# A selective scan on one core: two alternating sum banks, a delta preparation that borrows the idle one, and column sums with a standing vector of ones

## The chip, the core and the metric

The kernel runs on one core of one Trainium2 chip. The metric is the device time of one execution in microseconds, as the median of several runs. All float work is fp32 unless said otherwise; a few operands are fp8 or bf16. The engines are named as the profile names them: PE (matrix multiply) and PEld (its weight loads), DVE (vector), ACT (scalar), POOL (gpsimd) and SP (which issues nearly all DMAs). Each engine works through its own queue in the order of the program; semaphores order the engines against each other.

## The reference, cut to what matters

The input is an image batch of 4 x 64 x 64 x 96. Layer 0 normalizes it by groups, projects it to 192 channels with binarized weights, convolves, and then runs a selective scan over 4 directions for each image; layer 1 is a linear attention and a quantized feed-forward. Two parts are touched here. The first is the group mean, which needs the sum over all 4096 positions of each of 96 channels:

```python
m = jnp.mean(g, axis=(1, 2, 4), keepdims=True)      # inside _gn
return ((g - m) / jnp.sqrt(s + eps)).reshape(v.shape)
```

The second is the scan, for each image `b`, direction `k`, channel `d` (192) and state `n` (16), along 4096 positions:

```python
delta = jax.nn.softplus(delta + delta_bias[None, :, :, None])
dA = jnp.exp(dt[..., None] * A[None])
h = dA * h + (dt * ut)[..., None] * Bt[:, :, None, :]
y = jnp.einsum('bkdn,bkn->bkd', h, Ct)               # the sum over the 16 states
```

## The kernel before, in words

**Pieces.** The scan is cut into 1,536 pieces: 4 images x 4 directions x 4 chunks of 1024 positions x 6 groups of 32 channels x 4 quarters of 4 states. A piece is a tile of 128 rows (32 channels x 4 states) by 1024 positions. `Scans.run` (from line 1323) goes through the pieces with one loop; iteration `i` writes out, in this order, the instructions below, and each engine keeps its share of them in that order.

- `loads(i)`: SP issues broadcast loads of delta and delta times u (`dl`), and of the rows of B and C (`bc`), for later pieces.
- `carry(i-1)` (line 1271, ACT): the last column of piece i-1 is kept for the next chunk.
- `evacuate(i-4)` (line 1316, ACT, only when `i % 8 == 3`): the sums of the eight pieces 8m to 8m+7 are copied out of the bank `y` to `ys`, and four stores follow later.
- `decay(i+1)` (line 1231, ACT): exp(delta A) of the next piece, into `dA`, a pool of two buffers in the accumulator memory. Each buffer is free again when the piece two places back has been read.
- `reduce(i-3)` (lines 1302 and 1307, PE): eight recorded matmuls with `sum4` add the states of piece i-3 into the bank `y`; at the last quarter of a group up to two other directions are added too. A tile `y` collects eight pieces. The next tile takes the same bank, so `reduce(8m+8)` needs `evacuate` of the tile before.
- `inject(i+4)` (POOL): w = (delta u) B for the piece four places on, into one of nine buffers.
- `late_product()` and `scan(i)`: the recurrence is one DVE instruction, either in place in `dA` or, when the product with C is to be POOL's, into a buffer `h`. The product with C is DVE's or POOL's; a running tally of both engines' estimated work (`Tally`, line 389 on) decides which when the program is written. Both go through the helper line 401, so the profile tells them apart by tile names.
- One step of each open generator in `lanes`, then one step of `back`.

**Preparing delta.** Every eighth iteration (`i % 8 == 0`) opens one `prepare()` (from line 1149): delta and delta times u for a third of a chunk. Its steps, one in each iteration, are: eight matmuls into the bank `dps` (line 1167); Abs and Relu on ACT (1172, 1173); Exp and Ln on ACT (1175, 1176), Ln writing back into `dps`; the matmul that adds the Relu part (1179); the product with u on DVE; a copy on ACT (1185) and the stores. It also issues the load of u into `pu` (line 1157). Three preparations run ahead of the loop in borrowed tiles (`w_s`, `dA_s`).

**Banks.** The pool `ps` has four one-bank tiles: `y`, `dps`, and `b0`, `b1`, which `back` uses. The pool `dA` has the other half of the accumulator memory.

**What stands around the loop.** The weights are made (`weights`) in turns with the first image's `prologue` before the loop. `back` yields the rest of that prologue, then the prologues of the other images, the transposes of one direction (`turn`) and the attention and feed-forward of each finished image (`Epilogue`), one step in each iteration. The last image's epilogue runs after the loop.

**Column sums.** At the start of `prologue` 32 matmuls (line 510, two records each) take a block of x, 128 positions by 96 channels, as standing weights and a single column of ones as moving data; they add up in one column `csum`. Four steps hold eight matmuls each. Then ACT copies the column (514), a matmul adds the three channels of a group (`gsum`, 516), and ACT makes the negative mean (519).

Of the kernel before, what the change touches and what calls it, by code (L numbers as in the profile page):

```python
# [53 lines left out]
def hybrid_kernel(ctx: ExitStack, tc: tile.TileContext, a: dict, out: bass.AP):  # L54
# [102 lines left out]
    def weights():  # L157
# [28 lines left out]
        def transposed(dst, srcs):  # L186

            count[0] += 1
            ps = p.ps.tile([128, 1024], BF16, name=f"tps{count[0]}", tag=("y", "dps")[count[0] % 2])
            at = 0  # L190
            for src in srcs:
                n, f = src.shape
                nc.tensor.transpose(ps[:f, at : at + n], src, identb[:n, :n])
                at += n
            nc.vector.tensor_copy(dst, ps[:f, 0:at], saturate=False if dst.dtype == F8 else None)
# [152 lines left out]
        nc.vector.tensor_copy(  # L348
            back4.rearrange("p (x d) -> p x d", x=4), ident.rearrange("p (x d) -> p x d", x=4)[:, ::-1, :]
        )  # L350
        ps = p.ps.tile([128, 512], F32, name="tpd", tag="dps")
        for g in range(3):
            for x in range(4):
                nc.tensor.matmul(
# [122 lines left out]
def prologue(c, b, xts=None):  # L477
# [5 lines left out]
    def f32(nm):  # L483
        return p.f.tile([128, 512], F32, name=f"{nm}_{b}", tag="f")
# [4 lines left out]
    with tc.tile_pool(name=f"xg_{b}", bufs=1) as xgp:  # L489
# [3 lines left out]
        with tc.tile_pool(name=f"cv_{b}", bufs=1) as cvp:  # L493
# [6 lines left out]
            if xts is None:  # L500
# [4 lines left out]
                load_x(c, b, xts)  # L505
                yield
                yield
            csum = bank("csum", 0)[0:96, 0:1]
            for i in range(NT):
                nc.tensor.matmul(csum, xts[i // 8][:, i % 8, :], c.ones1, start=(i == 0), stop=(i == NT - 1))  # L510
                if i % 8 == 7:
                    yield
            cs = f32("cs")[0:96, 0:1]
            nc.scalar.copy(cs, csum)
            gsum = bank("gsum", 1)[0:96, 0:1]
            nc.tensor.matmul(gsum, c.grp, cs, start=True, stop=True)
            yield
            negm = f32("negm")[0:96, 0:1]
# [578 lines left out]
class Scans:  # L1097
# [19 lines left out]
    def done(self, b, n):  # L1117

        return self.at > (b * NK + n) * NPC + SETTLE


    def load_signs(self, b, k):

# [6 lines left out]
    def prepare(self, spare=None):  # L1130

        nc, c, p = self.c.nc, self.c, self.c.p
        b, k, ci, part = self.todo.pop(0)
        nm = f"{b}_{k}_{ci}_{part}"

        at = 16 * (NCH - 1 - ci if k >= 2 else ci)
        if (b, k) not in self.gs:  # L1140
            self.load_signs(b, k)
        if (ci, part) == (NCH - 1, 0) and k != KORD[-1]:
            self.load_signs(b, KORD[KORD.index(k) + 1])
        ud = (c.utd if k % 2 else c.ud)[b].rearrange("h p (n l) -> (h p) n l", l=IW)
        if part != 1:
            u = spare[2] if spare else p.pu.tile([128, CH], F32, name=f"pu_{nm}", tag="pu")
            if part == 0:
                cuts = ((slice(0, 128), slice(0, 128), slice(at, at + 16)),)
            else:
                lines = [slice(at + 8 * x, at + 8 * x + 8) for x in range(2)]  # L1150
                cuts = [
                    (slice(64 * x, 64 * x + 64), slice(128, DN), lines[1 - x if k >= 2 else x]) for x in range(2)
                ]
            n = 16 if part == 0 else 8
            v = u[:, 0 : 64 * n].rearrange("p (n l) -> p n l", l=IW)
            for rows, chans, lines in cuts:
                nc.sync.dma_start(v[rows], ud[chans, lines])
            self.us = v[:, ::-1, ::-1] if k >= 2 else v
        gT = self.gs[b, k]
        uv = self.us[:, 8 * part : 8 * part + 8] if part < 2 else self.us  # L1160
        d = spare[0] if spare else p.pd.tile([128, 2, 512], F32, name=f"pd_{nm}", tag="pd")
        ps = spare[3] if spare else p.ps.tile([128, 512], F32, name=f"dps_{nm}", tag="dps")
        pv = ps.rearrange("p (c q s) -> p s q c", q=4, s=8)
        groups = ((0, 128, 0, part),) if part < 2 else ((0, 64, 128, 0), (64, 64, 128, 1))
        wd, c0 = (c.wdz, 32 * ci + 16 * part) if part < 2 else (c.wdy, 32 * ci)
        for s in range(8):
            nc.tensor.matmul(pv[:, s], wd[:, k, s], gT[:, :, c0 : c0 + 16], start=(s == 0), stop=(s == 7))  # L1167
        yield
        kind = part // 2
        sc, bi = c.pvd[:, kind, k : k + 1], c.dbias[:, kind, k : k + 1]  # L1170
        t = spare[1] if spare else p.pd.tile([128, 512], F32, name=f"sp_{nm}", tag="sp", bufs=1)
        nc.scalar.activation(d[:, 0], ps, AF.Abs, scale=sc, bias=bi)  # L1172
        nc.scalar.activation(t, ps, AF.Relu, scale=sc, bias=bi)  # L1173
        yield
        nc.scalar.activation(d[:, 0], d[:, 0], AF.Exp, scale=-1.0)
        nc.scalar.activation(ps, d[:, 0], AF.Ln, bias=1.0)
        yield

        nc.tensor.matmul(ps, c.ident, t, start=False, stop=True, skip_group_check=True)  # L1179
        yield  # L1180
        c.vec.tensor_tensor(
            d[:, 1].rearrange("p (i j) -> p i j", j=64), ps.rearrange("p (i j) -> p i j", j=64), uv, ALU.mult
        )
        yield
        nc.scalar.copy(d[:, 0], ps)
        for x, (r0, n, d0, hf) in enumerate(groups):
            at = CH * ci + 512 * hf
            dst = c.dld[k][b][:, d0 : d0 + n, at : at + 512].rearrange("t d l -> d t l")
            then = (lambda: self.loaded.add((b, k, ci, part))) if x == len(groups) - 1 else None
            c.later.store(dst, d[r0 : r0 + n], after=1, then=then)  # L1190
# [102 lines left out]
    def reduce(self, i):  # L1293

        c = self.c
        b, e, ci, g, q = self.pieces[i]
        if i % 8 == 0:
            self.ydone[i // 8] = c.p.ps.tile([128, 2, 256], F32, name=f"yp_{i}", tag="y")
        y, prod = self.ydone[i // 8], self.ins.pop(i)
        more = self.sums.pop(i // NQ, []) if q == NQ - 1 else []  # L1300
        for x in range(4):
            c.nc.tensor.matmul(  # L1302
                y[32 * x : 32 * x + 32, g % 2, :], c.sum4, prod[:, 256 * x : 256 * x + 256],
                start=(q == 0), stop=(q == NQ - 1 and not more), tile_position=(0, 32 * x),
            )
        for n, (src, w) in enumerate(more):
            c.nc.tensor.matmul(y[:, g % 2, :], w, src, start=False, stop=(n == len(more) - 1))  # L1307
# [15 lines left out]
    def run(self, back):  # L1323
        c, lanes, n = self.c, [], len(self.pieces)

        w = [c.p.w.tile([128, CH], F32, name=f"w_s{x}", tag="w") for x in range(7)]
        ps = [c.p.dA.tile([128, CH], F32, name=f"dA_s{x}", tag="dA") for x in range(2)]
        for x in range(3):
            half = slice(512 * (x % 2), 512 * (x % 2) + 512)
            lanes.append(  # L1330
                self.prepare((
                    w[x].rearrange("p (t l) -> p t l", t=2), w[3 + x // 2][:, half], w[5 + x // 2], ps[x // 2][:, half],
                ))
            )
        interleave(lanes)
        for q in range(NQ):
            self.load_bc(0, self.bt, 0, 0, 0, q)
            self.load_bc(1, self.ct, 0, 0, 0, q)
        while lanes:
            interleave(lanes)  # L1340
            c.later.tick()
        c.later.flush()
        self.load_dl(0)
        for m in (1, 2):
            self.load_dl(m)
        self.decay(0)
        for i in range(AHEAD):
            self.inject(i)
        for i in range(n):
            self.at = i  # L1350
            self.loads(i)
            if i % NQ == 1:
                while KORD[self.pieces[i][1]] == 2 and self.pieces[i][0] not in c.turned:
                    next(back)
                self.load_sums(i)
            if i >= 1:
                self.carry(i - 1)
            if i % 8 == 3 and i > 8:
                self.evacuate(i - 4)
            if i + 1 < n:  # L1360
                self.decay(i + 1)
            if i >= 3:
                self.reduce(i - 3)
            if i + AHEAD < n:
                self.inject(i + AHEAD)
            self.late_product()
            self.scan(i)
            c.later.tick()
            if i % 8 == 0 and self.todo:
                while (self.todo[0][0], self.todo[0][1] % 2) not in c.ready:  # L1370
                    next(back)
                lanes.append(self.prepare())
            interleave(lanes)
            next(back, None)
            if i > n - 64:
                next(back, None)
        self.late_product()
        for i in range(n - 3, n):
            self.reduce(i)
        self.evacuate(n - 1)  # L1380
        c.later.flush()
        self.at = 2 * n
# [76 lines left out]
```

## Time and profile before

| | us |
|---|---|
| median of 6 runs | 5537.71 |
| lowest and highest of them | 5531.88 and 5540.85 |
| the profiled execution, its own time | 5541.11 |
| its span in the profile | 5539.3 |
| first scan starts, last scan starts (in the span) | 262.8 and 5414.9 |
| mean granted PE clock, share of full speed | 0.713 |

The profile is one execution. A group of the profile is a line, an engine, an operation and its tiles; it gives the busy time, the mean duration of one, and the idle time of that engine just before, with the event that ended it. The view of waits adds that idle time up by who waited for whom. The timeline gives single instructions with their start and duration in us. The table of windows gives the busy time of each engine in a stretch of the span.

### The profile page before, as it was taken

The page shows a single profiled execution, that of the slowest core. Times are in us where ns is not written, and L with a number is a line of the kernel's source. Part 1 is how long each engine was busy: PE and PEld are TensorE (multiplying, and loading weights), DVE is VectorE, ACT ScalarE, POOL GpSimd, SP SyncE. Part 2 cuts the span into 40 slices and gives each one's busy share as a digit, 9 for nine tenths or more (in the row PEclk, how much of TensorE's full clock was granted, in tenths as well). Part 3 has the DMA queues.
Part 4 walks back from the last instruction along what each step waited for, and adds up shares of the span by engine and source line. Part 5 has one row for each costly group of instructions (what it writes and reads, how often), then busy time and mean ns, then how long its engine had stood idle before and what let it go on. Part 6 is the DMA issues. An engine that isn't in the chain of part 4 may idle for free. (4 is left out here: it accounts for less than half of the span.)

```text
span 5539.3 us, 62371 instructions
## 1 busy us (share of the span) xinstructions
PE 3435.8 (62%) x20197; PEld 1357.9 (25%) x20197; DVE 5051.7 (91%) x3237; ACT 3556.4 (64%) x5564; POOL 4994.1 (90%) x2262
## 2 busy tenths in 40 slices
PE   6456655576557766568656775544676564444677
PEld 3222222222223222223222222111232121111223
DVE  3299999999999999899999999999999999999984
ACT  4467776777666667677766667755566775555554
POOL 2199999899999999899999999999999999999981
PEclk8667776678668876667777777656787776556777
DMA  4455666766666566767656556665665566665642
GB/s 80 124 184 191 206 198 194 250 200 200 210 211 196 192 203 206 222 207 219 205 191 205 189 194 207 218 204 192 216 215 187 187 200 201 212 208 189 206 151 60
DMA packets 613245, 1069.94 MB, mean 193 GB/s; under 512 B 225084, under 2 KB 343925, under 8 KB 611125
## 3 DMA queue, kind: packets, MB, share of 16 engines
q1 hardware_dynamic: 599428, 1065.88, 61.6%
q8 instruction: 159, 2.61, 0.2%
q10 hardware_dynamic: 13488, 0.07, 0.1%
q14 instruction: 170, 1.38, 0.1%
HBM read 833.20 MB, written 229.38 MB: 192 GB/s over the span
## 5 line engine op out<-in xcount | busy, mean ns | idle before, releaser
L401 POOL TENSOR_TENSOR w<-dl,bc 128x1024 f32<-128x1024 f32 x1536 | 3578.8, 2354 | 166.5 <-PE yp L1302 90.5
L1231 ACT ACTIVATE dA<-dl,anm 128x1024 f32<-128x1024 f32 x1536 | 1715.7, 1117 | 472.0 <-DVE w L401 289.5
L1302 PE MATMUL yp<-w,sum 128*32 128x256 f32 x12288 | 1260.2, 507 | 1083.8 <-ACT ys L1316 609.7
L401 DVE TENSOR_TENSOR_SCAN dA<-dA,cy,w 128x1024 f32<-128x1024 f32 x706 | 1654.4, 2343 | 95.0 <-ACT dA L1231 83.9
L401 POOL TENSOR_TENSOR w<-h,bc 128x1024 f32<-128x1024 f32 x596 | 1401.6, 2352 | 96.1 <-DVE h L401 88.4
L401 DVE TENSOR_TENSOR w<-dA,bc 128x1024 f32<-128x1024 f32 x940 | 1151.3, 1225 | 48.4 <-DMA bc<-bcd 0.8
L401 DVE TENSOR_TENSOR_SCAN h<-dA,cy,w 128x1024 f32<-128x1024 f32 x446 | 1043.3, 2340 | 9.7 <-ACT dA L1231 9.0
L1302 PEld LDWEIGHTS yp<-w,sum 128*32 128x32 f32 x12288 | 307.9, 127 | 2132.8 <-issue 688.4
L1271 ACT COPY cy<-dA 128x1 f32<-128x1 f32 x707 | 110.8, 157 | 691.6 <-DVE w L401 690.2
L401 DVE TENSOR_TENSOR_SCAN dA<-dA,w 128x1024 f32<-128x1024 f32 x234 | 534.2, 2283 | 21.9 <-ACT dA L1231 18.1
L577 PE MATMUL cv<-tp,cw 96*96 96x512 fp8e5 x1152 | 362.1, 458 | 80.3 <-ACT r L627 68.0
L401 DVE TENSOR_TENSOR_SCAN h<-dA,w 128x1024 f32<-128x1024 f32 x150 | 341.7, 2279 | 24.0 <-POOL w L401 23.5
L1179 PE MATMUL dps<-sp,ident 128*128 128x512 f32 x378 | 356.1, 1041 | 0.0
L1307 PE MATMUL yp<-ya,back 128*128 128x256 f32 x576 | 234.2, 527 | 0.0
L577 PEld LDWEIGHTS <-cw 96*96 96x96 fp8e5 x1152 | 158.8, 146 | 272.8 <-issue 218.8
L1271 ACT COPY cy<-h 128x1 f32<-128x1 f32 x445 | 82.7, 186 | 147.0 <-DVE h L401 146.0
L847 PE MATMUL yc<-eys,mean 96*96 96x512 f32 x240 | 135.7, 718 | 36.2 <-DVE vks L401 16.0
L1172 ACT ACTIVATE pd<-dps,dbias,pvd 128x512 f32<-128x512 f32 x189 | 143.8, 761 | 15.8 <-PE dps L1167 15.7
L1307 PEld LDWEIGHTS yp<-ya,back 128*128 128x128 f32 x576 | 121.9, 244 | 126.4 <-issue 96.2
L1173 ACT ACTIVATE sp<-dps,dbias,pvd 128x512 f32<-128x512 f32 x189 | 144.7, 766 | 0.0
L401 DVE TENSOR_TENSOR pd<-dps,pu 128x512 f32<-128x512 f32 x189 | 127.5, 675 | 5.1 <-PE dps L1179 4.8
L1316 ACT COPY ys<-yp 128x512 f32<-128x512 f32 x192 | 111.7, 582 | 29.3 <-PE yp L1307 18.7
(282 smaller groups left out, 4028.9 us busy)
## 6 DMA issues: line engine op xcount, KB each, us to landing
dl<-dld SPq DMA_DIRECT2D x768, 512.0 KB
bc<-bcd SPq DMA_DIRECT2D x512, 512.0 KB
dld<-pd SPq DMA_DIRECT2D x126, 512.0 KB
yd<-ys SPq DMA_DIRECT2D x768, 64.0 KB
dld<-pd SPq DMA_DIRECT2D x126, 256.0 KB
ya<-yd SPq DMA_DIRECT2D x192, 128.0 KB
pu<-ud SPq DMA_DIRECT2D x32, 512.0 KB
pu<-utd SPq DMA_DIRECT2D x31, 512.0 KB
```

The lines of the kernel that those rows point to most:

```text
L401: return getattr(self.eng, name)(out, *args, **kw)
L577: nc.tensor.matmul(ps, c.cw[:, j, t, 96 * h : 96 * h + 96], tpad[j][:, 8 * q + dy : 8 * q + dy + 8, dx : dx + IW], start=(j == 0 and t == ...
L847: self.c.nc.tensor.matmul(ps, w, x, start=(i == 0), stop=(i == len(pairs) - 1))
L1172: nc.scalar.activation(d[:, 0], ps, AF.Abs, scale=sc, bias=bi)
L1173: nc.scalar.activation(t, ps, AF.Relu, scale=sc, bias=bi)
L1179: nc.tensor.matmul(ps, c.ident, t, start=False, stop=True, skip_group_check=True)
L1231: c.nc.scalar.activation(t, self.dlt[i // NQ][0], AF.Exp, scale=c.anm[:, g, NQ * KORD[e] + q : NQ * KORD[e] + q + 1])
L1271: self.c.nc.scalar.copy(self.carries[g, q], h[:, CH - 1 : CH])
L1302: c.nc.tensor.matmul(y[32 * x : 32 * x + 32, g % 2, :], c.sum4, prod[:, 256 * x : 256 * x + 256], start=(q == 0), stop=(q == NQ - 1 and no ...
L1307: c.nc.tensor.matmul(y[:, g % 2, :], w, src, start=False, stop=(n == len(more) - 1))
L1316: c.nc.scalar.copy(t, y[:, :, ::-1] if k >= 2 else y)
```

## The change

- The tags `y` and `dps` become `y0` and `y1`. The sums of eight pieces go to `y0` and `y1` in turns (`i // 8 % 2`). `prepare` puts its `dps` tile into the bank that the sums do not use at that time (`bank()`).
- A preparation opens at `i % 8 == 3` and not at 0. It has one empty step more, after Exp and Ln, so that its last step (copy and stores) falls six iterations after its first.
- `evacuate(i-4)` is written after `decay(i+1)`; before, it was written ahead of it.
- A fourth preparation runs ahead of the loop, after the three first `dl` loads are issued and before `decay(0)`, in the tiles `w[7]`, half of `w[4]`, a `pu` tile and half of `ps[1]`.
- The column sums take the ones as standing weights (128 x 1) and 384 columns of x as moving data: eight matmuls in place of 32, two in each of four steps, into a row of 384. ACT copies the row, four small matmuls turn and add its four quarters into one column (`cst`), and a further step follows before `cs` is copied.
- In `weights`, the transposes and the `tpd` tile take `y0` and `y1` in turns.

```diff
-            ps = p.ps.tile([128, 1024], BF16, name=f"tps{count[0]}", tag=("y", "dps")[count[0] % 2])
+            ps = p.ps.tile([128, 1024], BF16, name=f"tps{count[0]}", tag=f"y{count[0] % 2}")
...
-            csum = bank("csum", 0)[0:96, 0:1]
-            for i in range(NT):
-                nc.tensor.matmul(csum, xts[i // 8][:, i % 8, :], c.ones1, start=(i == 0), stop=(i == NT - 1))
-                if i % 8 == 7:
+            csum = bank("csum", 0)[0:1, 0 : 4 * DM]
+            for i in range(0, NT, 4):
+                nc.tensor.matmul(
+                    csum, c.ones1, xts[i // 8][:, i % 8 : i % 8 + 4, :].rearrange("p i e -> p (i e)"),
+                    start=(i == 0), stop=(i == NT - 4),
+                )
+                if i % 8 == 4:
                     yield
+            row = f32("csr")[0:1, 0 : 4 * DM]
+            nc.scalar.copy(row, csum)
+            ps = bank("cst", 1)[0:96, 0:1]
+            for i in range(4):
+                nc.tensor.matmul(
+                    ps, row[:, DM * i : DM * i + DM], c.ones1[0:1, :], start=(i == 0), stop=(i == 3)
+                )
+            yield
             cs = f32("cs")[0:96, 0:1]
-            nc.scalar.copy(cs, csum)
-            gsum = bank("gsum", 1)[0:96, 0:1]
+            nc.scalar.copy(cs, ps)
+            gsum = bank("gsum", 0)[0:96, 0:1]
...
+    def bank(self):
+
+        return max(0, self.at - 3) // 8 % 2
...
-        ps = spare[3] if spare else p.ps.tile([128, 512], F32, name=f"dps_{nm}", tag="dps")
+        ps = spare[3] if spare else p.ps.tile([128, 512], F32, name=f"dps_{nm}", tag=f"y{1 - self.bank()}")
...
         nc.scalar.activation(ps, d[:, 0], AF.Ln, bias=1.0)
+        yield
         yield
...
-            self.ydone[i // 8] = c.p.ps.tile([128, 2, 256], F32, name=f"yp_{i}", tag="y")
+            self.ydone[i // 8] = c.p.ps.tile([128, 2, 256], F32, name=f"yp_{i}", tag=f"y{i // 8 % 2}")
...
-        w = [c.p.w.tile([128, CH], F32, name=f"w_s{x}", tag="w") for x in range(7)]
+        w = [c.p.w.tile([128, CH], F32, name=f"w_s{x}", tag="w") for x in range(8)]
...
+        u = c.p.pu.tile([128, CH], F32, name="pu_s", tag="pu")
+        for _ in self.prepare((w[7].rearrange("p (t l) -> p t l", t=2), w[4][:, 512:CH], u, ps[1][:, 512:CH])):
+            pass
         self.decay(0)
...
+            if i + 1 < n:
+                self.decay(i + 1)
             if i % 8 == 3 and i > 8:
                 self.evacuate(i - 4)
-            if i + 1 < n:
-                self.decay(i + 1)
...
-            if i % 8 == 0 and self.todo:
+            if i % 8 == 3 and self.todo:
```

More of the change, by code (lines that the diff above doesn't have):

```diff
@@ L350, in weights @@
         )
-        ps = p.ps.tile([128, 512], F32, name="tpd", tag="dps")
+        ps = p.ps.tile([128, 512], F32, name="tpd", tag="y0")
         for g in range(3):
```

## The prediction

> **What bounds the kernel now.** I read the page's busy times first, then the windows, the waits of DVE and of POOL inside the loop, and last the timeline. The first two fences are the page's first part and two rows of the table of windows (start and end, length, busy us of PE, PEld, DVE, ACT, POOL, PE clock, DMA share, GB/s).
>
> ```profile
> PE 3435.8 (62%) x20197; PEld 1357.9 (25%) x20197; DVE 5051.7 (91%) x3237; ACT 3556.4 (64%) x5564; POOL 4994.1 (90%) x2262
> ```
>
> ```profile
> 600.00:1600.00 1000.00, 624.61 (x4146) 258.14 (x4144) 957.57 (x588) 708.39 (x1098) 960.81 (x420) 0.70 0.67 206
> 1600.00:2600.00 1000.00, 679.05 (x3718) 257.89 (x3718) 954.94 (x596) 691.81 (x1089) 956.85 (x418) 0.73 0.65 205
> ```
>
> In the loop DVE and POOL are both busy 96% of the time; PE and ACT are not full. So the change, which removes no DVE or POOL work from the loop, can only win idle time of these two. The next two fences are the view of waits of DVE and of POOL between 400 and 5300 us (total us, times, longest).
>
> ```profile
> DVE dA L401 <- ACT dA L1231: 97.8, 84, 5.3
> ...
> DVE dA L401 <- ACT cy L1271: 9.8, 12, 1.3
> DVE h L401 <- ACT dA L1231: 8.2, 6, 3.2
> ...
> DVE dA L401 <- POOL w L401: 2.3, 5, 1.3
> ```
>
> ```profile
> POOL w L401 <- PE yp L1302: 77.2, 50, 6.9
> POOL w L401 <- DVE h L401: 76.0, 100, 2.0
> ```
>
> DVE waits for POOL 2.3 us in 4900, but for a late decay on ACT 97.8 + 8.2 = 106 us. POOL waits for PE 77.2 us and for DVE 76.0 us: it catches up, then waits for DVE again. So DVE sets the loop's time, and a stall of POOL costs nothing while DVE has injected pieces in stock. The price list of the change is what it does to those 106 us.
>
> The groups' view names a larger number, which is not on that path:
>
> ```profile
> L1302 PE MATMUL yp<-w,sum 128*32 128x256 f32 x12288 | 1260.2, 507 | 1083.8 <-ACT ys L1316 609.7
> ```
>
> PE stands 609.7 us before `reduce`, waiting for `evacuate`. What that does to DVE shows in the timeline (start, duration):
>
> ```profile
> 1001.40 1.08 ACT L756 COPY yh<-yt 96x512 f32<-96x512 f32 x1 [2.88 <-DMA yt<-yd]
> 1002.38 0.15 ACT L1271 COPY cy<-dA 128x1 f32<-128x1 f32 x1
> 1002.43 0.58 ACT L1316 COPY ys<-yp 128x512 f32<-128x512 f32 x1
> 1002.91 1.12 ACT L1231 ACTIVATE dA<-dl,anm 128x1024 f32<-128x1024 f32 x1
> ...
> 1003.07 1.08 PE L1302 MATMUL yp<-w,sum 128*32 128x256 f32 x8 [10.88 <-ACT ys L1316]
> ...
> 1004.14 2.35 DVE L401 TENSOR_TENSOR_SCAN h<-dA,cy,w 128x1024 f32<-128x1024 f32 x1 [2.17 <-ACT dA L1231]
> ```
>
> ACT is late, evacuates, and only then makes the decay that DVE waits for: 0.58 of DVE's 2.17 us is the evacuation. PE's 10.88 us delay nobody here.
>
> **Evacuation behind the decay.** I numbered the scans of the timeline and sorted DVE's waits for a decay by piece number modulo 8. Piece 4, whose decay stands behind the evacuation, has 27 of them and 26.2 us, the most of all. Eleven show the pattern above without a wait of ACT's own; each can win at most the copy's 0.58 us or its whole stall, together 6.0 us. In four more the evacuation itself waited (for PE or a load), and the whole stall goes: 0.66 + 0.79 + 0.82 + 0.99 = 3.3 us. In seven, 8.1 us together, the decay began only at the very end of the scan ahead of it (ACT's idle there ends with "DVE h"); an earlier decay may or may not escape that. I take half, 4.0 us. Sum: 6.0 + 3.3 + 4.0 = -13.3 us; bounds 0 (something else on ACT is late next) and -26.2.
>
> **Preparation moved by three iterations, with one step more.** It issues the same instructions: eight matmuls (0.29 us each), Abs and Relu 0.76 + 0.77, Exp and Ln 0.62 + 0.60, two matmul records of 1.04, a DVE product of 0.68, a copy of 0.58. Before, Abs to Ln stand in iterations 1 and 2, just before the evacuation in 3; afterwards the evacuation comes first and Abs to Ln stand in 4 and 5. Piece 3's stalls were 17.9 us, pieces 5, 6, 7 and 0 average 9.7 us; the excess of some 8 us should move to pieces 6 and 7. I take 0, bounds -8 and +8. The `pu` load, one of 512 KB or two of 128, now queues on SP behind two `dl` loads of 512 KB in the same iteration (those come at every `i % 4 == 3`). Its reader is the product five iterations later, 5 x 3.37 = 17 us, before four; DVE waited for `pu` 0.2 us in all. Cost 0.
>
> **Banks.** `reduce(8m+8)` no longer waits for the evacuation. But the preparation's first matmuls, in the same iteration, do: their bank is the one being emptied. PE's queue stops one instruction later, and the evacuation ends later by the decay's 1.12 us. Behind the stop were one reduce (1.08) and the 2.08 us of the Relu matmul; now eight matmuls of 1.03. So `reduce(8m+9)` comes some 1.08 + 2.08 - 1.12 - 1.03 = 1.0 us earlier, and POOL's 77.2 us should shrink, perhaps by half. DVE does not wait for POOL: 0, bounds 0 and -77.2. The new wait's queue: behind it on PE stand the step of `back` and later reduces; ACT's Abs, one iteration on, waits for these matmuls. Between evacuation and Abs ACT has at least a carry and a decay, 0.16 + 1.12 = 1.28 us, against 1.03 on PE. Taken as 0, bounds 0 and +30 (third rival).
>
> The Trainium skill ("Perfetto Trace Analysis", section Matmuls) says that independent groups of matmuls should rotate through banks so that an evacuation overlaps the next group. By that rule the 609.7 us were the prize, and the time 4931 us; by the waits of DVE above it is worth almost nothing, and I go by the waits.
>
> **Start of the loop.** The fourth preparation stands ahead of `decay(0)`. Its chain on its own is 1.0 + 1.5 + 1.2 + 1.8 + 0.7 + 0.6 = 6.8 us, but its product waits for a `pu` load behind six `dl` loads: 7 x 0.524 MB at 247 GB/s (window 253 to 262) from 254 us, so about 269. `decay(0)` comes at about 270 instead of 258.5, and the first scan at 271 instead of 262.8. The cover is POOL: its six injects run from 260.4 to 274.2, and only then does it take the first product. Cost 0; +4 if the load lands that much later.
>
> **Column sums.** Before, 64 records took 10.35 us at the start (31.87 to 42.22) and 4 x 2.7 in the loop. A 384-column fp32 record is not in the trace; a 512-column one is 0.445 us near the end and 1.04 in L1179's mean, so 0.33 to 0.78 for 384, and 5.3 to 12.5 us for 16 of them. At the start the gain is hidden: ACT's `negm` came at 44.26 us, 2 us after the sums, behind a weight step that waits for DMA and POOL. The longer chain (row copy about 0.5, eight short records, one step) puts the prologue one turn behind the weights; turns follow each other by some 1.3 us there (two copies of 0.67). I take +1.3 us, bounds -3 and +4. In the loop one late `csum` held ACT 8.4 us and DVE 5.3 us, once; that stays or goes: 0, bounds -5 and +3.
>
> **The sum.** -13.3 + 1.3 = -12.0 us on the profiled execution's 5541.1: 5529.1. That execution was 3.4 us above the median of 5537.7, so I predict 5526.
>
> **Rivals.**
> 1. *Nothing that can be measured (5538).* PE's wait moves from `reduce` to the preparation, and the decays are late for other causes: half of piece 4's stalls are not behind an idle-free evacuation. For it: the 8.1 us above. Against it: the order on ACT certainly changes. Gain 3 to 5, cost 1.3 to 4.
> 2. *More (5505).* Half of POOL's 77.2 us and the 12 us above come through, 5538 - 39 - 12 = 5487 at most; two thirds of it give 5505. For it: POOL is busy 96% as well and may bind in some stretches. Against it: DVE's 2.3 us.
> 3. *Slower: the stop of PE reaches ACT (5569).* Where ACT is late (27 of 192 blocks), PE starts the preparation 1.12 us later, Abs waits for it in the middle of ACT's queue, and the next decays wait behind Abs: 27 x 1.12 = 30 us, and no gain, +1.3. It decides once PE needs more than 1.28 us from evacuation to Abs; eight matmuls take 1.03 at the slow clock, so 0.25 us are left. Today Abs waits 15.8 us in all.
>
> **Numbers.** Forecast 0.45 (its own range 5512 to 5538), nothing 0.23, more 0.12, slower 0.20. What a measurement of this kernel can tell from no change is about 0.2%, 11 us. Faster by more than that (below 5526.6): 0.28 of the forecast and all of "more", 0.40; within it: 0.17 and 0.23, 0.40; slower 0.20. The range 5503 to 5566 leaves out half of "more" and some 0.12 of "slower".
>
> **What would show it.** Right: PE's wait for `ys` before L1302 falls from 609.7 us to under 60 and returns before L1167; DVE's waits at piece 4 fall from 26 us to 10 to 15; L1172's idle time stays under 40 us; POOL's wait for `yp` falls below 60; the first scan starts at about 271 us, the first product of POOL still near 274. Wrong: waits of DVE for decays at pieces 5 to 7 grow by as much as piece 4 loses (rival 1); L1172 waits 100 us or more for L1167 (rival 3); the loop starts later than 266 us on POOL.

## The result, and the profile after

The changed kernel takes 5553.99 us (median of 16 runs, 5547.84 to 5563.64), the kernel before 5538.58 us beside it (34 runs): ratio 1.0029, 95% interval [1.0022, 1.0035]. It is slower, by 15.4 us. The prediction said 5526 us, 12 us less than before. Its range, 5503 to 5566, holds the time, but only because the third rival had stretched it upwards, and that rival's mechanism did not occur (below). Its sign is wrong.

The profiled execution took 5548.84 us, with a span of 5547.1 us, 5 us below its kernel's median; that of before was 2.5 us above its own. So the profiles show only 7.7 of the 15.4 us (5547.1 - 5539.3). Line numbers after the change: decay 1248, carry 1288, evacuation 1333, `reduce` 1319, the preparation's matmuls 1183, Abs 1188, Relu 1189, Exp 1191, Ln 1192.

The page's first part, and the two windows (start and end, length, busy us of PE, PEld, DVE, ACT, POOL, PE clock, DMA share, GB/s):

```profile
PE 3463.0 (62%) x20037; PEld 1363.5 (25%) x20037; DVE 5053.1 (91%) x3237; ACT 3567.2 (64%) x5568; POOL 4996.1 (90%) x2262
```

```profile
600.00:1600.00 1000.00, 627.83 (x4091) 259.78 (x4089) 957.60 (x590) 709.86 (x1098) 960.41 (x419) 0.71 0.67 207
1600.00:2600.00 1000.00, 669.97 (x3680) 249.21 (x3679) 952.40 (x592) 691.88 (x1086) 955.70 (x418) 0.72 0.65 204
```

DVE, ACT and POOL are busy as before, to 0.3 points. The work did not change; only waits did. The mean granted PE clock was 0.707, against 0.713 before; DVE's waits that PE ended came to 16.6 us between 400 and 5300 us, against 18.9 before, so the clock did not carry the loss there. DVE's and POOL's waits between 400 and 5300 us:

```profile
DVE dA L401 <- ACT dA L1248: 99.4, 87, 3.7
DVE h L401 <- ACT dA L1248: 17.6, 9, 5.3
DVE dA L401 <- ACT cy L1288: 7.0, 8, 1.3
DVE dA L401 <- POOL w L401: 7.0, 7, 1.9
```

```profile
POOL w L401 <- DVE h L401: 106.1, 125, 2.9
POOL w L401 <- PE yp L1319: 46.9, 35, 4.4
```

DVE's wait for decays has grown, from 106.0 to 117.0 us (first two lines). POOL's wait for PE fell from 77.2 to 46.9 us, and its wait for DVE rose by as much, from 76.0 to 106.1. The groups of PE and of Abs (busy us, mean ns of one | idle us before them, and what ended it); the last line is Abs in the kernel before:

```profile
L1319 PE MATMUL yp<-w,sum 128*32 128x256 f32 x12288 | 1299.5, 518 | 448.9 <-POOL w L401 289.2
L1183 PE MATMUL dps<-gT,wdz 128*128 128x64 fp8e5 x1000 | 119.0, 323 | 444.1 <-ACT ys L1333 412.4
L1183 PE MATMUL dps<-gT,wdy 128*128 128x64 fp8e5 x504 | 56.7, 311 | 186.5 <-ACT ys L1333 186.5
L1188 ACT ACTIVATE pd<-dps,dbias,pvd 128x512 f32<-128x512 f32 x188 | 143.2, 762 | 18.1 <-PE dps L1183 17.9
...
L1172 ACT ACTIVATE pd<-dps,dbias,pvd 128x512 f32<-128x512 f32 x189 | 143.8, 761 | 15.8 <-PE dps L1167 15.7
```

`reduce` no longer stands for the evacuation (`ys`); the preparation's matmuls do, for 412.4 + 186.5 = 598.9 us. Abs waits 17.9 us for them, 15.7 before: PE's stop does not reach ACT.

**Where the time came from.** I summed DVE's idle time between scan 64 and the last scan from the timeline: 160.8 us before, 168.5 after, with DVE busy 4776.5 and 4777.7 us (idle time of less than 0.15 us at a stretch is counted as busy). The difference, 7.7 us, is as much as the span grew. The row that grew on ACT's side is its wait, ahead of a decay, for a scan into `h`; here before and after:

```profile
ACT dA L1231 <- DVE w L401: 272.1, 159, 2.8
ACT dA L1231 <- DVE h L401: 144.4, 118, 2.7
```

```profile
ACT dA L1248 <- DVE w L401: 279.6, 167, 2.9
ACT dA L1248 <- DVE h L401: 190.3, 150, 2.7
```

The second row rose from 144.4 us in 118 waits to 190.3 in 150. A timeline of after shows such a wait (start, duration; scan 637 is the one at 2416.59, into `h`):

```profile
2414.87 0.76 ACT L1188 ACTIVATE pd<-dps,dbias,pvd 128x512 f32<-128x512 f32 x1
2415.45 1.23 DVE L401 TENSOR_TENSOR w<-dA,bc 128x1024 f32<-128x1024 f32 x1
...
2416.59 2.34 DVE L401 TENSOR_TENSOR_SCAN h<-dA,cy,w 128x1024 f32<-128x1024 f32 x1
...
2417.52 0.15 ACT L1288 COPY cy<-dA 128x1 f32<-128x1 f32 x1
...
2418.96 1.12 ACT L1248 ACTIVATE dA<-dl,anm 128x1024 f32<-128x1024 f32 x1 [1.29 <-DVE h L401]
...
2420.18 2.36 DVE L401 TENSOR_TENSOR_SCAN dA<-dA,cy,w 128x1024 f32<-128x1024 f32 x1 [1.25 <-ACT dA L1248]
```

ACT is not late: after the carry at 2417.52 it has nothing ahead of decay 638, and stands 1.29 us until scan 637 has ended, at 2418.93. Then the decay takes 1.12 us, and DVE stands 1.25 us. Piece 636 was scanned in place and its product (2415.45) was done at 2416.68, so 636's `dA` buffer was free. But the program gave decay 638 the buffer of 637, the piece *just ahead*, which is read until 2418.93. The semaphore value that this decay waits for in the built program is the one that scan 637 raises.

I call these decays **tied**: the decay of piece k has the buffer of piece k-1 where k-2 is in place and k-1 goes into `h`. Then k-2's buffer always comes free first, since its product stands ahead of scan k-1 on DVE. The built program of before has 73 tied decays, that of after 93; only 22 pieces are tied in both. In the traces 63 and 88 of them begin within 0.08 us of the end of scan k-1, and DVE stands 54.4 and 79.6 us behind them. DVE's other waits for decays fell from 56.8 to 39.6 us. So -17.2 + 25.2 = +8.0 us: the other waits shrank by more than the forecast gain, and the tied decays grew by more than that. (A wait has one last cause, so part of the first is only the second in its place.)

### The profile page after: what moved, and what is told of

Its sections match the earlier page's. It is cut to its first block, busy times and chain, and to the rows that moved or that the text cites. A ratio compares the mean times of both kernels' runs of the same rounds, so it can differ in the third digit from the quotient of the medians.

```text
span 5547.1 us, 62051 instructions
## 1 busy us (share of the span) xinstructions
PE 3463.0 (62%) x20037; PEld 1363.5 (25%) x20037; DVE 5053.1 (91%) x3237; ACT 3567.2 (64%) x5568; POOL 4996.1 (90%) x2262
## 5 line engine op out<-in xcount | busy, mean ns | idle before, releaser
L1319 PE MATMUL yp<-w,sum 128*32 128x256 f32 x12288 | 1299.5, 518 | 448.9 <-POOL w L401 289.2
L401 DVE TENSOR_TENSOR_SCAN h<-dA,cy,w 128x1024 f32<-128x1024 f32 x447 | 1045.8, 2340 | 18.5 <-ACT dA L1248 17.9
L401 DVE TENSOR_TENSOR_SCAN dA<-dA,w 128x1024 f32<-128x1024 f32 x235 | 536.6, 2283 | 34.1 <-ACT dA L1248 28.1
L1183 PE MATMUL dps<-gT,wdz 128*128 128x64 fp8e5 x1000 | 119.0, 323 | 444.1 <-ACT ys L1333 412.4
L1196 PE MATMUL dps<-sp,ident 128*128 128x512 f32 x376 | 273.5, 817 | 60.2 <-ACT dps L1192 60.2
L1183 PEld LDWEIGHTS <-wdz 128*128 128x128 fp8e5 x1024 | 99.4, 156 | 526.8 <-issue 491.7
L1183 PE MATMUL dps<-gT,wdy 128*128 128x64 fp8e5 x504 | 56.7, 311 | 186.5 <-ACT ys L1333 186.5
L1188 ACT ACTIVATE pd<-dps,dbias,pvd 128x512 f32<-128x512 f32 x188 | 143.2, 762 | 18.1 <-PE dps L1183 17.9
```

What stands on the lines that cost most here:

```text
L401: return getattr(self.eng, name)(out, *args, **kw)
L1319: c.nc.tensor.matmul(y[32 * x : 32 * x + 32, g % 2, :], c.sum4, prod[:, 256 * x : 256 * x + 256], start=(q == 0), stop=(q == NQ - 1 and no ...
```

## The experiments

The first theory is that: the buffers that the pool `dA` hands out set the time; the change moves instructions on ACT, and with them the choice made when the program is written. The rivals: one part of the change costs by itself, through ACT's queue (the swap, the later preparation, the banks), or through the start (the column sums, the fourth preparation). Each expectation names its theories anew. The table behind the experiments gathers their numbers.

**1 and 2. Fixed buffers, in the kernel before and in the kernel after.** Each piece has the buffer of its parity, so no decay can be tied. (The other users of the pool get one of the two tags as well.)

```diff
-        t = c.p.dA.tile([128, CH], F32, name=f"dA_{i}", tag="dA")
+        t = c.p.dA.tile([128, CH], F32, name=f"dA_{i}", tag=f"dA{i % 2}", bufs=1)
```

> The kernel before, with one edit: the decay of an even piece always takes the first dA buffer, of an odd piece the second, so a decay always follows the piece two places back. In the trace of before 63 decays begin only at the end of the scan just ahead of them, with 54 us of DVE waiting behind them (88 decays and 80 us in the changed kernel). Theory 1 (a decay that is late on ACT is given the buffer of the piece just ahead, and that wait is the loss): no decay starts at that end any more, DVE's waits for decays fall from 111 to about 57 us, time 5538 - 35 to 54 = 5484 to 5503. Theory 2 (ACT is simply late in those places, whichever buffer is taken): DVE waits as long as before, 5530 to 5545.

> The changed kernel with the same edit, even and odd pieces each with a dA buffer of their own. Theory 1 (the loss of the change is the longer list of decays that take the buffer just ahead, 88 against 63 in the traces): DVE's waits for decays fall from 119 to about 40 us, 5554 - 60 to 80 = 5474 to 5494, and this kernel is 9 to 17 us faster than the kernel before with the same edit. Theory 2 (the preparation's Abs, Relu, Exp and Ln in iterations 4 and 5, right behind the evacuation, make decays of pieces 6 and 7 late in any case): 10 to 15 us slower than the kernel before with the same edit.

Measured: 5481.43 us, ratio to before 0.9901 [0.9887, 0.9914], and 5483.08 us, 0.9903 [0.9888, 0.9918]. The first kernel is a little faster than the first theory's range. Fixing the buffers takes off 1% or more of either kernel, and no difference between the two can be told any more. Of the second kernel's first theory, the time came true, but not the 9 to 17 us by which it should have been faster than the first; nor was it 10 to 15 us slower, as the second theory had it. DVE's waits for decays, in the kernel before with fixed buffers and then in the kernel after with fixed buffers:

```profile
DVE dA L401 <- ACT dA L1231: 53.7, 45, 5.5
...
DVE h L401 <- ACT dA L1231: 8.4, 5, 5.0
...
DVE dA L401 <- ACT cy L1271: 0.7, 1, 0.7
```

```profile
DVE dA L401 <- ACT dA L1248: 45.3, 38, 4.9
DVE h L401 <- ACT dA L1248: 20.7, 10, 5.5
```

62.1 and 66.0 us, against 106.0 and 117.0 with the pool's choice. ACT's wait of 144.4 us for scans into `h` is, in the first of these kernels:

```profile
ACT dA L1231 <- DVE h L401: 61.5, 64, 1.4
```

**3 and 4. The swap alone, and all of the change but the swap.**

```diff
+            if i + 1 < n:
+                self.decay(i + 1)
             if i % 8 == 3 and i > 8:
                 self.evacuate(i - 4)
-            if i + 1 < n:
-                self.decay(i + 1)
```

The third kernel is before with this edit; the fourth is after with its reverse.

> The kernel before with one part of the change alone: evacuate(i-4) is written after decay(i+1). Banks, phase of the preparation and column sums are those of before. The order of ACT hardly changes the list of decays that wait for the scan just ahead (75 in the program, 73 before). Theory 1: the evacuation's share of the waits at piece 4 goes, -5 to -10 us, 5528 to 5533. Theory 3 (the later evacuation itself holds up PE and with it the rest): 5548 to 5555, as the whole change.

> The changed kernel with that one part undone: evacuate(i-4) is again written ahead of decay(i+1). Theory 1: the waits from the moved preparation stay (86 decays in the program wait for the scan just ahead, 93 in the changed kernel) and the evacuation's share at piece 4 comes back: 5550 to 5562. Theory 3 (the later evacuation is the loss): 5535 to 5543.

Measured: 5534.40 us, 0.9998 [0.9989, 1.0007], and 5544.32 us, 1.0010 [1.0001, 1.0019]. Tied decays in the programs: 75 and 86. Both miss their ranges: the third lies above the 5528 to 5533 of its first theory, the fourth between the two ranges given for it. The swap alone does nothing that can be measured. Beside the rest of the change it costs: 1.0029 with it, 1.0010 without it, where the tied decays number 93 and 86. At 0.75 us each (worked out below) these seven come to 5 of the 10 us; what the other half is was not looked into.

**5 and 6. The preparation's shift alone, and the column sums alone.** The fifth is after with the old column sums, the evacuation first, and the banks `y` and `dps` of before; what is left is the opening at `i % 8 == 3`, the empty step and the fourth preparation ahead of the loop. The sixth is before with the new column sums.

```diff
-            self.ydone[i // 8] = c.p.ps.tile([128, 2, 256], F32, name=f"yp_{i}", tag=f"y{i // 8 % 2}")
+            self.ydone[i // 8] = c.p.ps.tile([128, 2, 256], F32, name=f"yp_{i}", tag="y")
...
-        ps = spare[3] if spare else p.ps.tile([128, 512], F32, name=f"dps_{nm}", tag=f"y{1 - self.bank()}")
+        ps = spare[3] if spare else p.ps.tile([128, 512], F32, name=f"dps_{nm}", tag="dps")
```

> One part of the change alone: the preparation opens at iteration 3 of eight, has its empty step and its fourth start ahead of the loop, but in a bank of its own; one bank for the sums, the evacuation ahead of the decay and the column sums as before. The four timed kernels without fixed buffers fit about 0.76 us for each decay that waits for the scan just ahead. The program of this one has 84 of them (73 before, 93 in the changed kernel). Theory 1 (moving ACT's work is what lengthens that list): 5538 + 11 x 0.76 = 5546, 5542 to 5550. Rival (the loss needs the shared bank, where PE stops for the evacuation): 5535 to 5541.

> The column sums with standing ones alone, in the kernel before. 75 decays of the program wait for the scan just ahead. Theory 1: 2 x 0.76 us and a turn of the prologue, 5538 to 5542. Rival (the column sums carry the loss): 5550 or more.

Measured: 5547.49 us, 1.0017 [1.0009, 1.0025], and 5540.98 us, 1.0002 [0.9993, 1.0012]. Tied decays: 84 and 75. Of the parts run alone, the shift of the preparation (with its fourth start ahead of the loop) is the one that makes the kernel slower; the column sums cost and gain nothing.

**7 and 8. Fixed buffers, and ACT's four steps of a preparation in four iterations.** The fifth kernel with fixed buffers, opened at 0 again, with Abs, Relu, Exp and Ln each in an iteration of its own. The seventh has the evacuation first, the eighth the decay.

```diff
         nc.scalar.activation(d[:, 0], ps, AF.Abs, scale=sc, bias=bi)
+        yield
         nc.scalar.activation(t, ps, AF.Relu, scale=sc, bias=bi)
         yield
         nc.scalar.activation(d[:, 0], d[:, 0], AF.Exp, scale=-1.0)
+        yield
         nc.scalar.activation(ps, d[:, 0], AF.Ln, bias=1.0)
         yield
-        yield
...
-            if i % 8 == 3 and self.todo:
+            if i % 8 == 0 and self.todo:
```

> Fixed dA buffers; banks, column sums and the place of the evacuation as in the kernel before; a preparation opens at iteration 0 of eight with the fourth ahead of the loop, and its Abs, Relu, Exp and Ln stand in four iterations in place of two. In the first experiment 62 us of DVE's waits for decays were left, 21 of them at piece 4. Theory 4 (what is left there comes from ACT's burst of four operations in two iterations, and the change only carried the burst to pieces 5 and 6): waits at piece 4 fall under 10 us, 5461 to 5474. Rival (they come from ACT waiting for PE and loads of the background steps): 5478 to 5486, as with fixed buffers alone.

> As the kernel with fixed buffers and the four operations in four iterations, and also the decay written ahead of the evacuation. Theory 4: a few us less than with the evacuation first, since with a spread burst only the copy's 0.58 us stands before the decay of piece 4: 5458 to 5472. Rival: no difference between the two, 5478 to 5486.

Measured: 5472.19 us, 0.9877 [0.9862, 0.9892], and 5468.74 us, 0.9873 [0.9856, 0.9891]. The eighth has the lowest median of all, 1.3% below the kernel before. Against fixed buffers alone (0.9901 [0.9887, 0.9914]) the gain is 0.2 to 0.3%, with intervals that overlap a little; both kernels also have the fourth preparation ahead of the loop, which fixed buffers alone had not. Piece 4's stalls in the seventh were 18.3 us, not the under 10 that I had expected of it, so the time fell as theory 4 said but its reason is not shown; in the eighth they were 8.8 us. Between the two no difference can be told.

**9 and 10. Fixed buffers, with the swap alone and with the shift alone.** The edits of 1 and 3, and of 1 and 5.

> Fixed dA buffers in the kernel before, and the decay written ahead of the evacuation; nothing else of the change. It sizes the first term of the prediction without the waits for the scan just ahead. With fixed buffers alone the time was 5481 (ratio 0.9901), and DVE waited 21 us for decays at piece 4. If the evacuation's place is worth what the prediction said, 5468 to 5475; if DVE only waits a little later (piece 4 less, piece 6 more, as in the kernel with the swap alone), 5477 to 5484.

> Fixed dA buffers, and the preparation moved to iteration 3 with its empty step and its fourth start; own bank, evacuation first, old column sums. Without fixed buffers the same move cost 0.17%. Theory 1: with them it costs nothing, 5477 to 5485. Theory 2 (ACT late in itself): 5487 to 5493.

Measured: 5492.54 us, 0.9916 [0.9902, 0.9930], and 5493.07 us, 0.9912 [0.9896, 0.9927]. Both miss what I expected of the buffers alone, by 8 us or more, and do not come down to the 5481 us of fixed buffers alone; the tenth lies at the upper edge of what the other theory gave it (5487 to 5493). The intervals overlap with that of fixed buffers alone, so each part may cost 0.1% through ACT's queue by itself, or nothing; the whole change with fixed buffers (0.9903) does not show it. This stays open. The swap gains nothing here either: piece 4's stalls went from 21.1 to 11.6 us, those of all pieces from 62.2 only to 59.2, and DVE's whole idle time in the loop rose from 108.8 to 118.6 us.

**11 and 12. Tied decays made on purpose.** With fixed buffers, the listed pieces get the buffer of the piece just ahead. In the eleventh, the kernel before, the list has the 73 that were tied there and 73 others; in the twelfth, the kernel after, 93 pieces of which none was tied there.

```diff
-        t = c.p.dA.tile([128, CH], F32, name=f"dA_{i}", tag=f"dA{i % 2}", bufs=1)
+        t = c.p.dA.tile([128, CH], F32, name=f"dA_{i}", tag=f"dA{(i + sum(k <= i for k in BEHIND)) % 2}", bufs=1)
```

> The kernel before with fixed dA buffers, but 146 decays are given the buffer of the piece just ahead on purpose: the 73 that had it in the kernel before, and 73 others, evenly spread over the remaining pieces whose predecessor is scanned into h and whose second predecessor is scanned in place. Theory 1 (each such decay costs what it cost before, (5538 - 5481) / 73 = 0.78 us): 5481 + 146 x 0.78 = 5595 us, ratio to the kernel before about 1.010; DVE some 100 to 120 us behind such decays. Theory 2 (the fixed buffers gain by something else, and the decays in question only go with it): 5481 to 5495 us, ratio 0.990 to 0.992. Theory 3 (only the places where the program put them cost, added ones fall where ACT has time): 73 x 0.78 and nothing for the others, 5538 us, ratio 1.000.

> The kernel after with fixed dA buffers, and 93 decays given the buffer of the piece just ahead: as many as in the kernel after, but none of the same pieces; they are evenly spread over the other pieces of the same kind, without the heap at pieces 6 and 7 of eight (15 of 93 there, 41 in the kernel after). Theory 1 (the number counts, at 0.76 us each): 5483 + 93 x 0.76 = 5554 us, ratio 1.003. Theory 2 (something else in the fixed buffers): 5483 to 5497 us, ratio 0.990 to 0.993. Theory 3 (their place counts, next to Abs, Relu, Exp and Ln): about half the cost, some 5520 us, ratio 0.997.

Measured: 5621.77 us, 1.0150 [1.0136, 1.0164], and 5586.29 us, 1.0084 [1.0070, 1.0098]. The cost comes back with the tied decays and with nothing else, so theories 2 and 3 fall. Theory 1 has the direction but not the size: 27 and 32 us more than it said. ACT's and DVE's waits in the eleventh:

```profile
ACT dA L1245 <- DVE h L401: 316.3, 182, 5.2
```

```profile
DVE dA L401 <- ACT dA L1245: 146.5, 141, 4.1
DVE dA L401 <- ACT cy L1285: 18.7, 20, 1.3
```

ACT's wait goes 61.5, 144.4, 316.3 us for 0, 73 and 146 tied decays in the same kernel. DVE's wait for the carry, behind the late decay on ACT, comes with it: 18.7 us, against 9.8 in the kernel before and 0.7 with fixed buffers.

**All of them together.** Tied decays by the built program; those that began at the end of scan k-1 in the trace, and DVE's idle us behind these; DVE's idle us from scan 64 to the last; the ratio to before.

| kernel | tied | in the trace | DVE idle behind them | DVE idle in the loop | ratio |
|---|---|---|---|---|---|
| before | 73 | 63 | 54.4 | 160.8 | 1 |
| after | 93 | 88 | 79.6 | 168.5 | 1.0029 |
| 3 swap alone | 75 | 69 | 55.0 | 154.7 | 0.9998 |
| 4 all but the swap | 86 | 77 | 71.6 | 163.8 | 1.0010 |
| 5 shift alone | 84 | 75 | 64.3 | 169.9 | 1.0017 |
| 6 column sums alone | 75 | 64 | 51.5 | 160.5 | 1.0002 |
| 1 before, fixed | 0 | 0 | 0 | 108.8 | 0.9901 |
| 2 after, fixed | 0 | 1 | 1.2 | 117.4 | 0.9903 |
| 9 swap, fixed | 0 | 2 | 0.7 | 118.6 | 0.9916 |
| 10 shift, fixed | 0 | 0 | 0 | 124.3 | 0.9912 |
| 7 four steps, evacuation first | 0 | 3 | 3.4 | 103.1 | 0.9877 |
| 8 four steps, decay first | 0 | 1 | 1.1 | 101.7 | 0.9873 |
| 11 before, 146 on purpose | 146 | 139 | 122.0 | 228.9 | 1.0150 |
| 12 after, 93 others on purpose | 93 | 94 | 90.8 | 199.2 | 1.0084 |

DVE is busy 4770 to 4785 us in the loop in all fourteen; most of what differs between them is its idle time. The 73 tied decays of before cost (1 - 0.9901) x 5538 / 73 = 0.75 us each, the 93 of after (1.0029 - 0.9903) x 5538 / 93 = 0.75. By this price the 20 that the change adds, net, are 15 us of the 15.4 measured.

That sum holds as far as kernels 1 and 2 take the same time, and each of their intervals reaches some 8 us to either side. In their profiles DVE idles 8.6 us longer in the second than in the first, as much as the 7.7 us between before and after, and in the ninth and tenth 9.8 and 15.5 us longer than in the first. So a part of the loss may come from the moved work on ACT itself, without any tie. That tied decays cost time is shown; that they are all of the 15.4 us is not.

## Why the prediction was wrong, step by step

**What bounds the kernel: right.** DVE's waits set the time and POOL's do not; the table's last two columns go together to 0.3%.

**The step that failed** is in the term "Evacuation behind the decay", which was to give -13.3 us and gave about -1 alone, and in the term "Preparation moved", which was put at 0 and cost 9 us alone. In the first it is the reading of piece 4's stalls, where in seven of them, 8.1 us, the decay "began only at the very end of the scan ahead of it", and which I counted at half their length. I saw the tie and took it for a remainder of one term. It was 54.4 of DVE's 111.2 us, over all pieces, and it was the largest single cause of waits. The account of the kernel even says that a buffer is free when the piece two places back has been read; for 73 decays that is not so, and asking which wait such a decay has in the program would have shown it. Because the tie depends on where the program writes ACT's work, it also made the term "preparation moved" wrong: 0, bounds -8 and +8. The shift alone measured +0.17% [0.09, 0.25], 9 us, with 84 tied decays for 73. The stalls it moved went where I said, to pieces 6 and 7, and more came with them: by piece number modulo 8, in us,

| | 0 | 1 | 2 | 3 | 4 | 5 | 6 | 7 | sum |
|---|---|---|---|---|---|---|---|---|---|
| before | 17.9 | 24.1 | 4.3 | 17.9 | 26.2 | 6.6 | 9.4 | 4.8 | 111.2 |
| after | 13.7 | 4.7 | 13.1 | 9.1 | 11.1 | 16.1 | 34.1 | 17.1 | 119.2 |
| before, fixed | 9.7 | 15.6 | 0 | 8.1 | 21.1 | 3.8 | 1.8 | 2.0 | 62.2 |

Of the 93 tied decays of after, 41 are at pieces 6 and 7, whose decays now follow Abs to Ln on ACT; of the 73 before, 24 were at pieces 3 and 4, which had that place then. The heap at piece 6 is not made by ties alone: with fixed buffers and no tie it is 22.4 us in the second kernel and 20.8 in the tenth, against 1.8 in the first. The prediction's own sign of being wrong, pieces 5 to 7 growing by as much as piece 4 loses, came out threefold: piece 4 lost 15 us, pieces 5 to 7 gained 46.

**Evacuation behind the decay (-13.3): piece 4 as forecast, the worth wrong.** Piece 4 fell to 11.1 us, inside the forecast 10 to 15. But alone the swap measured 0.9998 [0.9989, 1.0007], -1 us give or take 5. In its profile DVE's waits for decays fell by 22.6 us (111.2 to 88.6) and its whole idle time only by 6.1; waits for PE (31.2 to 40.4 us), POOL and loads took up most of the rest. The step that fails here is that a shorter wait for a decay is time won: the value was the lower end of the bounds, 0. The first rival named that value, but for another reason, decays late for other causes.

**Banks (0): as forecast, but not run alone.** The fourth kernel is the fifth with the banks and the column sums: 1.0010, against 1.0017 and 1.0002 for these two, which leaves nothing that can be measured for the banks. PE's wait moved from `reduce` to the preparation, 609.7 to 598.9 us. POOL's wait for PE fell by 30 us and nobody gained. The rotation through banks that the Trainium skill asks for ("Perfetto Trace Analysis", section Matmuls) is what the change does with the sums; here PE stood as long as before, one instruction later in its queue, and with fixed buffers the kernel with the rotation and the rest of the change (0.9903) and that without them (0.9901) take the same time. In this kernel PE does not bound the loop; what the rotation is worth where it does, no run here shows.

**Third rival: refuted.** It needed 100 us of waits ahead of Abs; there are 17.9. The kernel did become slower, but by another mechanism; the 0.20 given to "slower" stood for a cause that did not occur.

**Start of the loop (0): right.** The fourth preparation's product, the first decay, the first scan and POOL's first product:

```profile
266.57 0.69 DVE L401 TENSOR_TENSOR w_s<-dA_s,pu_s 128x512 f32<-128x512 f32 x1 [19.24 <-DMA pu_s<-utd]
...
267.77 2.16 ACT L1248 ACTIVATE dA<-dl,anm 128x1024 f32<-128x1024 f32 x2
269.00 4.47 DVE L401 TENSOR_TENSOR_SCAN h<-dA,w 128x1024 f32<-128x1024 f32 x2 [1.74 <-ACT dA L1248]
...
272.96 2.35 POOL L401 TENSOR_TENSOR w<-h,bc 128x1024 f32<-128x1024 f32 x1
```

The first scan is 6.2 us later than before (262.8), POOL's first product is near the forecast 274, and at scan 64 the lag has shrunk to 0.4 us: the cover held.

**Column sums (+1.3): nothing.** The records at the start:

```profile
31.66 7.30 PE L511 MATMUL csum<-xt,ones 128*1 128x384 f32 x16
...
42.45 1.40 PE L521 MATMUL cst<-ones,csr 1*96 1x1 f32 x8
```

16 records take 7.30 us, in the forecast 5.3 to 12.5, where 64 took 10.35; the longer chain behind them takes it back, and the negative mean on ACT comes at 44.62 us, before at 44.26. Alone they measure 1.0002 [0.9993, 1.0012].

**What stays open.** Why the pool gives the buffer just ahead in 73 or 93 cases was not looked into; only what it costs. The profile of after shows half of the median's loss, and its split by causes holds for that execution. Whether the swap or the shift alone costs 0.1% with fixed buffers, and so how much of the 15.4 us is not due to ties, is not settled.

## What to carry to other kernels

Where an engine in front of the bounding one waits while nothing in its own queue holds it up, look up which buffer it waits for: a pool of two that is thought to alternate may not, and fixing the buffer of each piece by its parity was worth 1% here, more than every move of work on ACT. As long as that is not fixed, a move of instructions also redraws the list of such waits (in the four kernels with parts of the change from 73 to 75, 86, 84 and 75), so a small effect of a move is to be measured with the buffers fixed. And price a move by the whole idle time of the bounding engine: stalls that left one place came back at others.

## What the runs showed beyond that

A tied decay has no single price. Where the program itself tied them it was 0.75 us each (interval about 0.1 either way); 146 in the kernel before cost (1.0150 - 0.9901) x 5541 / 146 = 0.95 us, and 93 others in the kernel after (1.0084 - 0.9903) x 5541 / 93 = 1.08 us. In the traces of these four kernels DVE stands 0.86 to 0.97 us behind each that shows there. That the program's own ties fall where other work on ACT is late anyway, which would make them cheaper, is my reading and not shown.
